# Four graph layers on one core: node terms split into eight gated stages, own rings for the float32r copies, score rows sent by chunk

## The chip, the cores and the metric

The kernel runs on one core of a Trainium2 chip. The metric is the device time of one execution in microseconds (us). Before the change three runs took 3625.14, 3625.96 and 3626.26 us; the median is 3625.96 us. Five engines work side by side, each through its own queue in order: TensorE (PE, with weight loads shown as PEld), VectorE (DVE), ScalarE (ACT), GpSimd (POOL) and SyncE (SP), which here only issues DMAs. POOL issues DMAs too.

## What is computed

x is 3327 x 512, adj a 3327 x 3327 0/1 matrix. Each of four layers normalises the rows, applies a relu, and adds its result to x. Layers 0 to 2 are graph attention with 8, 4 and 8 heads; layer 1 sets the self-loops; layer 3 is a mean over the neighbours with dense weights. Cut to what matters:

```python
h = jnp.maximum(_layernorm(x, axis=-1), 0.0)
Wh = h @ W                                   # per head
f1, f2 = (Wh * a1).sum(-1), (Wh * a2).sum(-1)
e = leaky_relu(f1[:, None] + f2[None, :], 0.2)
att = softmax(where(adj > 0, e, -big), axis=-1)   # layer 1: adj + eye
x = x + elu(att @ Wh)
# layer 3
agg = (adj > 0) @ h / max(deg, 1)
x = x + relu(concat([h @ Ws + bs, agg @ Wn + bn]) @ Wc + bc)
```

## The kernel before

The 3327 rows are 26 tiles of 128; four tiles make a chunk (seven chunks, the last has two). A leaky relu of a sum is one of two products, exp(f1)exp(f2) or its 0.2 power, so attention is two masked sums: of "positive" and of "negative" pairs. A head of a chunk goes like this in `attention` (L540). ACT, and DVE for some columns, compares the row scores s1b with a column's own (L593, L590) and writes 0/2 as fp8. DVE ands it with the mask (L599) and, in layers 0 and 2, makes the other half by xor (L603). PE multiplies these 128 x 128 weights with the exponentiated node terms (`ab`, three bf16 pieces of 65 columns each; L631, L634). Two row tiles `k` are one pass; a head has two passes.

Layer 1 has four heads and takes the positive sum (a = 0) and the negative one (a = 1) in separate passes, 16 a chunk. Its 26 columns lie in five groups of kinds "bssvv": group 0 is multiplied in bf16 (L627), groups 1 and 2 are turned to float32r by ACT, groups 3 and 4 by DVE (`real`, L522, copy at L527), and then multiplied at L624. All four copies of a pass use one ring `t6` of four slots. Between a = 0 and a = 1 DVE flips the masks' half in place (L659).

While layer l attends to chunk c, the rows of chunk c - 1 are finished and become terms of layer l + 1. That is done by `Hooks` (L502): after each pass `run` pushes every flying tile one stage further, starts a new tile every third hook (every hook in the last chunk), and in layer 0 loads one or two blocks of the mask (`load_mask`, L202). A tile's stages (`node_stages`, L428) are: `s0`, finish the row (L727 to L731), statistics on DVE (L301, L303), three small POOL steps (L304 to L306) and the relu on ACT (L308); a stage with nothing; `s1`, four PE transposes (L137) and the copy `hT` on ACT (L141); `s2`, `project` (L351): 8 float32 matmuls (L362), clipped scores (L363), two exponentials on ACT (L369, L370), products (L373) and the pieces on DVE, ACT and POOL (L335 to L341, or L381 and L382); `s3`, the stores and `send_s1` (L420), which transposes one tile's scores (L423), copies them (L425) and writes 8 or 4 rows to DRAM (L426). The head's load at L561 reads them back for 128 partitions.

The framework's scheduler sets the order of each engine's queue from the order of issue, the data dependences, its own notion of durations, and the extra edges that `after` (L144) adds; such an edge orders instructions and is no wait on the chip. `gone` holds the last matmul of each pass.

`open_layer` (L254) is called in the second head of chunk 0. It loads the next layer's weights and folds the two score vectors into them: eight times a product (L291) and a sum (L292), for layers 1 and 2 all on DVE. `mask_tiles` (L231) loads a chunk's masks in the head before the last; for layer 1 POOL copies the self-loop blocks into them at once (L243). Before the first pass of layer 0 the 26 tiles pass through the same stages with nothing beside them but mask loads (the first 172 us, "the lead-in" below).

Of the kernel before, what the change touches and what calls it, by code (L numbers as in the profile page):

```python
# [37 lines left out]
P = 128  # L38
# [14 lines left out]
def tile_gnn(ctx: ExitStack, tc: tile.TileContext, x, adj, W0, a01, W1, al, ar, W2, a2,  # L53
# [48 lines left out]
    s1d = [dram.tile([H, NT * P], F32, name=f"s1_{l}") for l, H in enumerate(heads)]  # L102
# [31 lines left out]
    def transposed(src, pool, name, bufs=2, behind=None):  # L134
        tp = ps.tile([P, KC, P], F32, name="tp", bufs=2)
        for k in range(KC):
            tr = nc.tensor.transpose(tp[:, k, :], src[:, k * P:(k + 1) * P], ident)  # L137
            if k == 0 and behind:
                after(tr, behind)
        dst = pool.tile([P, KC, P], F32, name=name, bufs=bufs)  # L140
        nc.scalar.copy(dst, tp)  # L141
        return dst
# [8 lines left out]
    stats = []  # L151

# [78 lines left out]
    def mask_tiles(c, self_loops=False, early=False):  # L231
        t0, nt = chunks[c]
        tiles = []
        for g, (j0, nj) in enumerate(JG):
            m = mk.tile([P, PER * JM * P], FP8, name="m")
            v = m[:, :nt * nj * P].rearrange("p (k j i) -> p k j i", k=nt, j=nj)
            ld = nc.sync.dma_start(v, maskd[c][g])
            if early and c == 0:
                after(ld, stored[21])
            if self_loops:  # L240
                for k in range(nt):
                    if j0 <= t0 + k < j0 + nj:
                        nc.gpsimd.tensor_copy(v[:, k, t0 + k - j0, :].bitcast(U32), dg1[:, t0 + k, :].bitcast(U32))  # L243
            tiles.append(v)
        return tiles
# [8 lines left out]
    def open_layer(l):  # L254
        L = Layer()
        L.l = l
        L.to_store = []
        if l == 3:
            L.w = []
            for i in range(2):  # L260
                w = pre.tile([P, KC, 2 * WW], F32, name="w")[:, :, :D]
                after(nc.sync.dma_start(w, Xd[i].rearrange("(c p) o -> p c o", p=P)), stored["gate"])
                L.w.append(w)
            return L
        H = heads[l]
        DK = D // H
        H2 = H // 2

        w = pre.tile([P, KC, 2 * WW], F32, name="w")[:, :, :2 * (D // 2 + H)]
        L.w = w.rearrange("p c (f o) -> p c f o", f=2)  # L270
        av = []
        for i in range(2):
            av.append(pre.tile([P, 2, H2, DK], F32, name="h"))
            ld = nc.sync.dma_start(av[i].rearrange("p f h d -> p (f h) d"), a_srcs[l][i].partition_broadcast(P))
            if l:
                after(ld, stored["gate"])
        for k in range(KC):
            for f in range(2):
                dst = L.w[:, k, f, :D // 2]
                if l == 0:  # L280
                    nc.sync.dma_start(dst.rearrange("p (g o) -> p g o", g=H2),
                                      W0[f * H2:(f + 1) * H2, k * P:(k + 1) * P, :].rearrange("h p o -> p h o"))
                else:
                    W = (W1, W2)[l - 1]
                    ld = nc.sync.dma_start(dst, W[k * P:(k + 1) * P, f * (D // 2):(f + 1) * (D // 2)])
                    if l:
                        after(ld, stored["gate"])
        for i in range(2):
            for k in range(KC):
                pr = pre.tile([P, 2, H2, DK], F32, name="e" if l or i else "AB", bufs=1)  # L290
                (nc.gpsimd if l == 0 and i else nc.vector).tensor_mul(pr, L.w[:, k, :, :D // 2].rearrange("p f (g o) -> p f g o", g=H2), av[i])  # L291
                nc.vector.tensor_reduce(L.w[:, k, :, D // 2 + i * H2:D // 2 + (i + 1) * H2], pr, AX.X, ALU.add)  # L292
        L.ks2 = pre.tile([P, NT, H], F32, name="ks2")
        L.ns2 = pre.tile([P, NT, H], F32, name="ns2")
        L.s12 = pre.tile([P, NT, 2, H], F32, name="s12", bufs=1)
        nc.vector.memset(L.s12, 0.0)
        return L

    def norm(xt, pool):
        st = pre.tile([P, 6], F32, name="st")  # L300
        nc.vector.bn_stats(st, xt)  # L301
        mv = pre.tile([P, 4], F32, name="mv")
        stats.append(nc.vector.bn_aggr(mv[:, 0:2], st).ins.name)  # L303
        nc.gpsimd.tensor_scalar(mv[:, 2:3], mv[:, 1:2], EPS, None, op0=ALU.add)  # L304
        nc.gpsimd.tensor_tensor(mv[:, 2:3], mv[:, 2:3], neghalf, ALU.pow)
        nc.gpsimd.tensor_scalar(mv[:, 3:4], mv[:, 0:1], mv[:, 2:3], -1.0, op0=ALU.mult, op1=ALU.mult)  # L306
        h = pool.tile([P, D], F32, name="h", bufs=2)
        nc.scalar.activation(h, xt, AF.Relu, bias=mv[:, 3:4], scale=mv[:, 2:3])  # L308
        return h
# [7 lines left out]
    def pieces(L, t, AB, pool, first):  # L317
# [17 lines left out]
        nc.vector.tensor_sub(r, AB, high(AB))  # L335
        for a in range(2):
            nc.scalar.copy(dst(0, a), high(AB[:, a]))
# [13 lines left out]
    def project(L, t, hT, pool, first):  # L351

        l, n = L.l, pn(t)
        c, kk = where[t]
        g, jj = jwhere[t]
        H, DA, AO, HW = dims(l)
        DK, H2 = DA - 1, H // 2
        pws = []
        for f in range(2):
# [3 lines left out]
            nc.vector.tensor_scalar(L.s12[:n, t, :, f * H2:(f + 1) * H2],  # L363
# [3 lines left out]
        s2 = L.s12[:, t, 1, :]  # L367
        AB = pool.tile([P, 2, H, DA], F32, name="AB", bufs=2 if first else 1)
        nc.scalar.activation(AB[:, 0, :, DK], s2, AF.Exp)  # L369
        nc.scalar.activation(AB[:, 1, :, DK], s2, AF.Exp, scale=SLOPE)  # L370
        for f in range(2):
# [3 lines left out]
                                 AB[:, :, hs, DK:DA].to_broadcast([P, 2, H2, DK]))  # L375
        if l == 1 and KIND[g] != "b":
            for f in range(2):
# [3 lines left out]
                nc.scalar.copy(v[:, 0], AB[:, :, hs])  # L381
# [3 lines left out]
        else:  # L385
            pieces(L, t, AB, pool, first)
        if t == JG[g][0] + JG[g][1] - 1:
            js = slice(JG[g][0], t + 1)
            nc.vector.tensor_scalar(L.ks2[:, js], L.s12[:, js, 1, :], BIG, None, op0=ALU.mult)
            nc.vector.tensor_scalar(L.ns2[:, js], L.s12[:, js, 1, :], -1.0, None, op0=ALU.mult)  # L390
# [29 lines left out]
    def send_s1(L, t, pool, first):  # L420
        H = heads[L.l]
        tps = ps.tile([H, P], F32, name="mm" if first else "tp", bufs=2)
        nc.tensor.transpose(tps, L.s12[:, t, 0, :], ident)  # L423
        s1t = pool.tile([8, P], F32, name="s1t", bufs=2)
        nc.scalar.copy(s1t[:H], tps)  # L425
        (nc.sync if first else nc.gpsimd).dma_start(s1d[L.l][:, t * P:(t + 1) * P], s1t[:H])  # L426

    def node_stages(L, t, get_x, pool, first=False):  # L428
# [4 lines left out]
        def s0():  # L433
            q["h"] = norm(get_x(), pool)

        def s1():
            behind = (L.mm if t == NT - 1 and not first else gone[-1]) if gone else None
            q["hT"] = transposed(q["h"], mp, "A", A_BUFS[2], behind) if late else transposed(q["h"], pool, "hT", 2, behind)

        def s2():  # L440
            if L.l == 3:
                project_last(L, t, q["hT"], 1)
            else:
                project(L, t, q["hT"], pool, first)

        def s3():
            if L.l != 3:
                for to, pt in L.to_store:
                    nc.sync.dma_start(to, pt)
                L.to_store = []  # L450
                send_s1(L, t, pool, first)
            elif late:
# [3 lines left out]
        return [s0, s1, s2, s3] if first else [s0, lambda: None, s1, s2, s3]  # L456

    def close_terms(L):
# [3 lines left out]
        s2v = L.s12[:, :, 1, :].rearrange("p t h -> p h t")  # L462
# [21 lines left out]
        s1v = L.s12[:, :, 0, :]  # L484
# [14 lines left out]
    class Hooks:  # L499


        def __init__(self):  # L502
            self.masks, self.tiles, self.flying, self.done = [], [], [], 0

        def run(self, every, n, masks=1):
            for st in list(self.flying):
                st.pop(0)()
                if not st:
                    self.flying.remove(st)
            if self.tiles and n % every == 0:  # L510
# [11 lines left out]
    def real(a, g, ks, th):  # L522
# [3 lines left out]
        t = mp.tile([P, 2, JM, P], F32R, name="t6", bufs=4)  # L526
# [13 lines left out]
    def attention(L, hooks, open_next, close):  # L540
# [5 lines left out]
        for c, (t0, nt) in enumerate(chunks):  # L546
# [4 lines left out]
            for h in range(H):  # L551
# [9 lines left out]
                nc.sync.dma_start(s1b[:, :W], s1d[l][h, t0 * P:t0 * P + W].partition_broadcast(P))  # L561
# [19 lines left out]
                for g, (j0, nj) in enumerate(JG):  # L581

                    pt = mp.tile([P, PER * JM * P], FP8, name="tht", bufs=11 if l == 1 else 7)
# [24 lines left out]
                for a in range(2 if l == 1 else 1):  # L608
# [5 lines left out]
                    for ks, js in passes:  # L614
# [40 lines left out]
                        hooks.run(1 if last else 3, hook, 2 if hook % 2 and c == 0 or hook % 3 == 0 and c else 1)  # L655
                        hook += 1
                    if a == 0:
                        for pu, mu in flip:
                            nc.vector.tensor_tensor(pu, pu, mu, ALU.bitwise_xor)  # L659
                if c == 0 and h == 0:  # L660
# [14 lines left out]
                if h == H - 2 and not last:  # L675
                    while l == 0 and hooks.done < (t0 + nt + chunks[c + 1][1]) * len(JG):
                        hooks.masks.pop(0)()
                    nmasks = mask_tiles(c + 1, l == 1)
# [74 lines left out]
    with tc.tile_pool(name="first", bufs=1) as fp:  # L753
# [21 lines left out]
        while hooks.tiles or hooks.flying:  # L775
# [8 lines left out]
            [A[1], ("ab", JM * 258, F32R, 7), R, ("t6", 2 * JM * P, F32R, 4), tht[:3] + (11,)],  # L784
# [533 lines left out]
```

## Time and profile before

| what | value |
|---|---|
| median of the runs | 3625.96 us |
| the profiled execution | 3629.69 us |
| its span, first to last instruction | 3627.9 us |
| around the span | 1.8 us |
| mean granted TensorE clock | 0.987 |
| matmuls | 31348 |
| lead-in, layer 0 | 0 to 172.5 us, 172.5 to 1181 us |
| layer 1, layer 2 | 1266 to 2080 us, 2167 to 3200 us |
| layer 3 after the last node terms | 3302 to 3627.9 us |

In the profile a line of a group names the source line, the engine, the operation, the tile written and the tiles read, then the count, the busy time and the mean duration. "Idle before" is time in which that engine stood still, and the arrow names what ended it. A matmul's shown duration includes its way through the array; the next one starts before it ends, so the pace is read from runs of them: 40 float32r matmuls of 258 columns take 5.10 us in a row.

### The profile page before, as it was taken

What the parts mean: (1) busy time and instruction counts of PE and PEld (TensorE: products, weight loads), DVE (VectorE), ACT (ScalarE), POOL (GpSimd) and SP (SyncE); (2) the same over time, 40 slices, a digit from 0 to 9 for tenths busy, and PEclk for the clock granted to TensorE, in tenths of its full rate; (3) what the DMA queues carried; (4) which work ended last, traced back from release to release, by engine and by line L of the source; (5) the groups of instructions that cost most, each with busy time, mean ns of one, the idle gap of its engine ahead of it and who ended that gap; (6) DMA issues with size and microseconds to landing.
All of it is one profiled execution on the core that took longest, in us unless ns stands there. A gap on an engine that the chain in (4) does not pass through costs nothing. (4 is left out here: it accounts for less than half of the span.)

```text
span 3627.9 us, 78882 instructions
## 1 busy us (share of the span) xinstructions
PE 3479.3 (96%) x31348; PEld 3143.1 (87%) x31348; DVE 2642.1 (73%) x5227; ACT 2517.0 (69%) x4170; POOL 620.6 (17%) x893
## 2 busy tenths in 40 slices
PE   7799999999999999999999989999999999999998
PEld 5699999999999888888888869989898989886886
DVE  7788888888887789878878858767776767672221
ACT  5778787778787889878888757767666767572211
POOL 6601221202010202223123230001010101011000
PEclk9999999999999999999999999999999999999999
DMA  7777677777766877767767885545555555586331
GB/s 217 238 211 233 203 234 214 219 220 237 220 200 212 290 270 280 245 247 268 261 246 254 293 290 204 193 168 189 181 184 172 201 176 174 166 284 250 105 106 52
DMA packets 322106, 780.72 MB, mean 215 GB/s; under 512 B 37122, under 2 KB 144645, under 8 KB 321088
## 3 DMA queue, kind: packets, MB, share of 16 engines
q1 hardware_dynamic: 292480, 713.17, 57.8%
q0 software_dynamic: 29248, 62.42, 7.1%
q8 instruction: 249, 4.08, 0.4%
q14 instruction: 129, 1.06, 0.1%
HBM read 667.96 MB, written 129.64 MB: 220 GB/s over the span
## 5 line engine op out<-in xcount | busy, mean ns | idle before, releaser
L631 PE MATMUL acc<-ab,tht 128*128 128x195 bf16 (+1 forms) x10816 | 1845.3, 248 | 14.9 <-DVE tht L599 12.0
L634 PE MATMUL acc<-ab,gt 128*128 128x195 bf16 (+1 forms) x10816 | 1844.8, 248 | 10.5 <-ACT gt L593 6.1
L593 ACT ACTIVATE gt<-s1b,ks 128x512 fp8e4<-128x512 f32 (+1 forms) x2464 | 1456.3, 677 | 250.2 <-issue 144.3
L634 PEld LDWEIGHTS <-gt 128*128 128x128 fp8e4 x10816 | 1061.2, 98 | 32.2 <-issue 16.1
L631 PEld LDWEIGHTS <-tht 128*128 128x128 fp8e4 x10816 | 1061.5, 98 | 25.4 <-DVE tht L599 13.3
L624 PE MATMUL acc<-ab,t 128*128 128x258 f32 x4160 | 547.5, 290 | 33.3 <-ACT t L527 29.4
L624 PEld LDWEIGHTS acc<-ab,t 128*128 128x128 f32 x4160 | 522.8, 193 | 47.1 <-ACT t L527 34.2
L599 DVE TENSOR_TENSOR tht<-gt,m 128x768 uint32<-128x768 uint32 (+3 forms) x560 | 447.2, 799 | 143.3 <-ACT gt L593 140.6
L603 DVE TENSOR_TENSOR gt<-tht,m 128x768 uint32<-128x768 uint32 (+3 forms) x560 | 446.8, 798 | 8.2
L527 ACT CAST t<-tht 128x1536 fp32r<-128x1536 fp8e4 x208 | 300.0, 1468 | 60.1 <-DVE tht L659 29.9
L730 POOL TENSOR_TENSOR xt<-xt,e 128x512 f32<-128x512 f32 x72 | 114.0, 1583 | 1240.6 <-DVE e L729 1198.7
L854 PE MATMUL acc<-y,mf 128*128 128x512 f32 x1352 | 309.8, 391 | 1.5 <-DVE mf L849 1.5
L593 ACT ACTIVATE tht<-s1b,ks 128x512 fp8e4<-128x512 f32 (+1 forms) x504 | 306.8, 679 | 1.8 <-DMA s1b<-s 1.8
L590 DVE TENSOR_SCALAR gt<-s1b,ns 128x512 fp8e4<-128x512 f32 (+1 forms) x448 | 213.5, 479 | 123.9 <-PE acc L634 123.8
L854 PEld LDWEIGHTS acc<-y,mf 128*128 128x128 f32 x1352 | 253.6, 188 | 57.6 <-DVE mf L849 1.9
L649 DVE TENSOR_REDUCE R<-acc 128x130 f32<-128x390 f32 x416 | 214.4, 554 | 70.4 <-PE acc L634 69.7
L851 ACT CAST mf<-m 128x768 fp32r<-128x768 fp8e4 (+1 forms) x78 | 59.1, 762 | 244.9 <-PE acc L854 233.1
L627 PE MATMUL acc<-ab,tht 128*128 128x387 bf16 x1248 | 225.2, 329 | 3.9 <-DMA ab<-ab 2.2
L362 PE MATMUL mm<-w,hT 128*128 128x260 f32 (+1 forms) x832 | 199.3, 392 | 13.5 <-ACT hT L141 10.9
L362 PEld LDWEIGHTS mm<-w,hT 128*128 128x128 f32 x832 | 156.8, 194 | 38.5 <-ACT hT L141 11.8
L627 PEld LDWEIGHTS <-tht 128*128 128x128 fp8e4 x1248 | 118.4, 98 | 80.7 <-DMA ab<-ab 2.2
L339 POOL TENSOR_TENSOR pt<-r 128x520 bf16<-128x520 f32 (+1 forms) x116 | 136.0, 1192 | 285.0 <-DVE r L335 282.6
(139 smaller groups left out, 3164.9 us busy)
## 6 DMA issues: line engine op xcount, KB each, us to landing
ab<-ab SPq DMA_DIRECT2D x336, 600.0 KB
ab<-ab SPq DMA_DIRECT2D x224, 400.0 KB
ab<-ab SPq DMA_DIRECT2D x112, 774.0 KB
ab<-ab SPq DMA_DIRECT2D x112, 516.0 KB
ab<-ab SPq DMA_DIRECT2D x56, 582.0 KB
s1b<-s SPq DMA_DIRECT2D x120, 256.0 KB
m<-mask SPq DMA_DIRECT2D x72, 384.0 KB
ab<-pt SPq DMA_DIRECT2D x13, 1600.0 KB
```

The source lines that it names most:

```text
L362: L.mm = nc.tensor.matmul(pw, hT[:, k, :], L.w[:, k, f, :], start=(k == 0), stop=(k == KC - 1)).ins.name
L527: (nc.scalar.copy if KIND[g] == "s" else nc.vector.tensor_copy)(t[:, :k1 - k0, :nj], th[a][g][:, k0:k1])
L590: nc.vector.tensor_scalar(gv[:, :, jj, :], s1v, L.ns2[:, j, h:h + 1], 2.0, op0=ALU.is_gt, op1=ALU.mult, saturate=False)
L593: nc.scalar.activation(gv[:, :, jj, :], s1v, AF.Relu, bias=L.ks2[:, j, h:h + 1], scale=BIG, saturate=False)
L599: nc.vector.tensor_tensor(pu, gu, mu, ALU.bitwise_and)
L603: nc.vector.tensor_tensor(gu, pu, mu, ALU.bitwise_xor)
L624: mm = nc.tensor.matmul(acc[k][:, :2 * DA], thr[g][:, k - ks[0], jj, :], ab[a][g][:, jj, :], start=(j == 0), stop=(j == NT - 1), skip_grou ...
L627: mm = nc.tensor.matmul(acc[k][:, :3 * DA], th[a][g][:, k, jj, :], ab[a][g][:, jj, :3 * DA], start=(j == 0), stop=(j == NT - 1), skip_grou ...
L631: nc.tensor.matmul(acc[k][:, :3 * DA + o], th[0][g][:, k, jj, :], ab[0][g][:, jj, :3 * DA + o], start=(j == 0), stop=False, skip_group_che ...
L634: mm = nc.tensor.matmul(acc[k][:, AO:AO + 3 * DA + o], th[1][g][:, k, jj, :], ab[0][g][:, jj, AO:AO + 3 * DA + o], start=False, stop=(j == ...
L649: nc.vector.tensor_reduce(R[:, k], v.rearrange("p a (s d) -> p a d s", s=3), AX.X, ALU.add)
L854: nc.tensor.matmul(acc[k], mf[:, jj, :], y2[g][:, jj, s, :], start=(j0 + jj == 0 and s == 0), stop=(j0 + jj == NT - 1 and s == 1))
```

## The change

1. A node tile has eight stages in layers 0 to 2 (six where the next layer is 3): load and finish; statistics; relu; transposes; projection; exponentials and products; pieces; send. From the second on they carry an `after` edge to the last pass's last matmul on their leading instructions (not on every one: the second exponential and the `hT` copy have none). In a layer's last chunk two stages are run per hook.
2. `send_s1` acts once a chunk: one transpose of up to 32 score rows, one copy, one DMA. The scores' DRAM tile is now `[tile, head, row]`, so the read for a head takes 512-byte pieces where it took 2048-byte ones.
3. The eight folds of layers 1 and 2 go one per hook.
4. Layer 1's ring `t6` of four becomes `ts` (three slots, ACT) and `tv` (two smaller slots, DVE); `tht` goes from 11 slots to 10.
5. Layer 1's self-loop copies are issued after the last head's passes.

```diff
-    s1d = [dram.tile([H, NT * P], F32, name=f"s1_{l}") for l, H in enumerate(heads)]
+    s1d = [dram.tile([NT, H, P], F32, name=f"s1_{l}") for l, H in enumerate(heads)]
...
             if self_loops:
                 for k in range(nt):
                     if j0 <= t0 + k < j0 + nj:
-                        nc.gpsimd.tensor_copy(v[:, k, t0 + k - j0, :].bitcast(U32), dg1[:, t0 + k, :].bitcast(U32))
+                        loops.append((v[:, k, t0 + k - j0, :].bitcast(U32), dg1[:, t0 + k, :].bitcast(U32)))
...
+    def set_loops(loops, behind=None):
+        for to, d in loops:
+            cp = nc.gpsimd.tensor_copy(to, d)
+            if behind:
+                after(cp, behind)
...
+        def fold(i, k):
+            pr = pre.tile([P, 2, H2, DK], F32, name="e" if l or i else "AB", bufs=1)
+            m = (nc.gpsimd if l == 0 and i else nc.vector).tensor_mul(
+                pr, L.w[:, k, :, :D // 2].rearrange("p f (g o) -> p f g o", g=H2), av[i])
+            if gone:
+                after(m, gone[-1])
+            nc.vector.tensor_reduce(L.w[:, k, :, D // 2 + i * H2:D // 2 + (i + 1) * H2], pr, AX.X, ALU.add)
+        folds = [lambda i=i, k=k: fold(i, k) for i in range(2) for k in range(KC)]
+        if l:
+            hooks.small = folds
...
-        tps = ps.tile([H, P], F32, name="mm" if first else "tp", bufs=2)
-        nc.tensor.transpose(tps, L.s12[:, t, 0, :], ident)
-        s1t = pool.tile([8, P], F32, name="s1t", bufs=2)
-        nc.scalar.copy(s1t[:H], tps)
-        (nc.sync if first else nc.gpsimd).dma_start(s1d[L.l][:, t * P:(t + 1) * P], s1t[:H])
+        tps = ps.tile([PER * H, P], F32, name="mm" if first else "tp", bufs=2)
+        nc.tensor.transpose(tps[:nt * H], L.s12[:, 0, t0:t0 + nt, :].rearrange("p t h -> p (t h)"), ident)
+        s1t = pool.tile([PER * 8, P], F32, name="s1t", bufs=2)
+        nc.scalar.copy(s1t[:nt * H], tps[:nt * H])
+        (nc.sync if first else nc.gpsimd).dma_start(s1d[L.l][t0:t0 + nt].rearrange("t h p -> (t h) p"), s1t[:nt * H])
...
-        return [s0, s1, s2, s3] if first else [s0, lambda: None, s1, s2, s3]
+        if first:
+            return [lambda: (q.update(x=get_x()), statistics(), relu()), turn,
+                    lambda: parts(L, t, scaled(L, t, projected(L, t, q["hT"], first), pool, first), pool, first), send]
+        stages = [lambda: q.update(x=get_x()), statistics, relu, turn]
+        if L.l == 3:
+            return stages + [lambda: project_last(L, t, q["hT"], 1), own]
+        return stages + [lambda: q.update(pw=projected(L, t, q["hT"], first)),
+                         lambda: q.update(AB=scaled(L, t, q["pw"], pool, first, behind())),
+                         lambda: parts(L, t, q["AB"], pool, first, behind()), send]
...
-        def run(self, every, n, masks=1):
+        def run(self, every, n, masks=1, steps=1):
             for st in list(self.flying):
-                st.pop(0)()
+                for _ in range(min(steps, len(st))):
+                    st.pop(0)()
                 if not st:
                     self.flying.remove(st)
+            if self.small:
+                self.small.pop(0)()
...
-        t = mp.tile([P, 2, JM, P], F32R, name="t6", bufs=4)
+        t = mp.tile([P, 2, nj, P], F32R, name="ts" if KIND[g] == "s" else "tv", bufs=3 if KIND[g] == "s" else 2)
...
-                    pt = mp.tile([P, PER * JM * P], FP8, name="tht", bufs=11 if l == 1 else 7)
+                    pt = mp.tile([P, PER * JM * P], FP8, name="tht", bufs=10 if l == 1 else 7)
...
-                        hooks.run(1 if last else 3, hook, 2 if hook % 2 and c == 0 or hook % 3 == 0 and c else 1)
+                        hooks.run(1 if last else 3, hook, 2 if hook % 2 and c == 0 or hook % 3 == 0 and c else 1, 2 if last else 1)
...
+                if h == H - 1 and not last:
+                    set_loops(pending, gone[-2])
```

## The prediction

> **What bounds the kernel.** First the page's busy shares, then the busy time of each engine by stage (columns: stretch, length, then busy time and instructions of PE, PEld, DVE, ACT, POOL, then granted clock, DMA share, GB/s).
>
> ```profile
> PE 3479.3 (96%) x31348; PEld 3143.1 (87%) x31348; DVE 2642.1 (73%) x5227; ACT 2517.0 (69%) x4170; POOL 620.6 (17%) x893
> ```
>
> ```profile
> 0.00:172.50 172.50, 125.24 (x650) 101.28 (x650) 129.26 (x253) 107.81 (x242) 117.27 (x193) 0.96 0.77 227
> 172.50:1181.00 1008.50, 986.57 (x11236) 968.91 (x11236) 839.82 (x1676) 791.63 (x1363) 166.56 (x258) 0.99 0.73 219
> ...
> 1266.00:2080.00 814.00, 781.64 (x5597) 680.95 (x5597) 682.89 (x1274) 667.19 (x918) 183.83 (x215) 0.98 0.73 262
> 2080.00:2167.00 87.00, 71.58 (x419) 56.74 (x417) 54.37 (x121) 49.00 (x86) 32.02 (x48) 0.95 0.91 329
> 2167.00:3200.00 1033.00, 1030.80 (x10731) 942.89 (x10732) 750.91 (x1482) 719.20 (x1199) 81.18 (x119) 1.00 0.54 183
> ```
>
> PE sets the time; layer 2 is PE without a hole (2.2 us idle). So only three things count: PE work removed, PE idle time, and time in which PE's clock is cut. Idle: 47.3 us in the lead-in, 21.9 in layer 0, 32.4 in layer 1, 15.4 between layers 1 and 2. The waits of PE within layer 1 (total, times, longest):
>
> ```profile
> PE acc L624 <- ACT t L527: 26.0, 12, 4.4
> PE acc L624 <- DVE t L527: 3.6, 5, 0.9
> ```
>
> Layer 1 waits for float32r copies. The timeline at one chunk end shows why; ACT's rows, then PE's:
>
> ```profile
> 1590.48 0.82 ACT L308 ACTIVATE h<-xt,mv 128x512 f32<-128x512 f32 x1 [3.88 <-POOL mv L306]
> 1591.20 4.39 ACT L593 ACTIVATE tht<-s1b,ks 128x512 fp8e4<-128x512 f32 x7
> ...
> 1595.69 2.54 ACT L593 ACTIVATE tht<-s1b,ks 128x512 fp8e4<-128x512 f32 x4
> 1598.14 1.15 ACT L337 COPY pt<-AB 128x520 bf16<-128x520 bf16 x2
> 1599.18 1.46 ACT L527 CAST t<-tht 128x1536 fp32r<-128x1536 fp8e4 x1
> 1600.55 1.15 ACT L341 COPY pt<-r 128x520 bf16<-128x520 bf16 x2
> ```
>
> ```profile
> 1600.70 2.11 PE L624 MATMUL acc<-ab,t 128*128 128x258 f32 x12 [3.04 <-ACT t L527]
> ```
>
> ACT stands 3.88 us at a node's relu that POOL has not prepared, then does 11 compares for a later head and two node copies, and only then the cast that PE needs. The same happens at five chunk ends (waits of 4.4, 3.0, 4.1, 4.1 and 2.9 us, 18.5 together). Over the five 20 us stretches around them PE is busy 81.13 of 100 us, and each has a granted clock of 0.91, another 1.8 us lost: 18.9 + 9.0 = 28 us.
>
> **The clock.** After the 3.04 us wait, 1600.60 to 1605.20 ran at 0.63; after a 5.69 us wait, 224.0 to 229.7 ran at 0.51. So a gap of 3 us costs about 1.7 us more. [...]
>
> **The change, part by part.**
>
> *Gated stages and own rings, layer 1.* The ring first. With one ring of four, the cast of group 1 in pass n waits for the last matmul on group 1 in pass n - 1. From there PE has 28 float32r matmuls (groups 2 to 4) and the 12 of bf16: 40 in 5.10 us gives 0.12 each, 12 in 2.14 us gives 0.16, so 3.4 + 2.0 = 5.4 us of cover. With three slots for ACT alone, the cast of group 2 waits for group 1 of the pass before: another 12 x 0.12, 6.8 us; that of group 1 has 10.7. DVE's cover stays at 5.8. Then the load: in the order of the old program the fullest steady interval between ACT's pairs of casts holds 11 compares, four piece copies, a relu, two exponentials and the casts. At the timeline's paces (0.61, 0.52, 0.72, 0.10, 1.37) that is 12.4 us, plus the 3.88 us idle; PE's pass lasts some 8.0 us (40 x 0.12 + 12 x 0.16, and a sixteenth of four nodes' 4.4 us). 12.4 - 8.0 = 4.4 is more than 5.4 less one cast, 3.9. In the order of the new program the fullest steady one has 12 compares, an exponential and the casts, 10.2 us: 2.2 late against 6.8 - 1.5 = 5.3. The relu stands a hook behind its statistics, so the 3.88 us wait should go too. So the chunk ends should close. I leave 4 of the 28 us: **-24**. Of the other 26.0 - 18.5 + 3.6 = 11.1 us of copy waits I take half, since DVE's ring gains nothing: **-5.5**. Ends for both: 0 and -39.
>
> *Folds.* In layer 0 DVE does eight folds in one go:
>
> ```profile
> 221.36 0.67 DVE L292 TENSOR_REDUCE w<-e 128x4 f32<-128x512 f32 x1
> 221.96 0.41 DVE L665 TENSOR_TENSOR R<-R 128x260 f32<-128x260 f32 x1
> 222.30 0.68 DVE L291 TENSOR_TENSOR e<-w,h 128x512 f32<-128x512 f32 x1
> 222.90 0.16 DVE L667 TENSOR_SCALAR rc<-R 128x4 f32<-128x4 f32 x1
> 222.97 0.95 DVE L603 TENSOR_TENSOR gt<-tht,m 128x768 uint32<-128x768 uint32 x1
> ```
>
> The xor at 222.97 that PE needs (it resumes at 224.06 after 5.69 us) stood behind them; they are 8 x (0.68 + 0.67) = 10.8 us. One per hook, 1.35 us in a pass of 8.7, hides in DVE's idle share. Gone: 5.7 us and half of the 5.7 us at 0.51, 2.8: **-8.5** (ends 0 and -8.5). Layer 1's folds cause no row of waiting.
>
> *Score rows by chunk.* 78 transposes become 21, in layers 1 and 2 52 become 14. Four L137 transposes take 0.60 us and one alone 0.27, so a further one costs 0.11: 38 x 0.11 = **-4**. The copies (0.25) and DMA issues (0.53 on POOL) that go lie off PE. The read back has 512 packets of 512 bytes for 128 of 2048; in the trace's packets these take 27 and 84 ns, so 140 loads cost (13.8 - 10.8) x 140 / 16 = 26 us more of each DMA engine's 3628, and each is asked for a head ahead: 0. If a head waited for its row, the nearest row is ACT's wait for s1b, 1.8 us in two times; ends 0 and +5.
>
> *Lead-in.* PE waits 10.0 us before score transposes and 8.8 (16 times) for hT, for the copy stood behind two exponentials; in the new order it mostly stands ahead of them. But between 40 and 120 us the DMA share is 0.82 to 1.01 and DVE busy 73 of 80 us: these set the pace. **-4**, ends 0 and -19.
>
> *Smaller pieces.* `tht` 11 to 10: one group fewer ahead; nearest row the 0.96 us L599 of 27 heads, ends 0 and +26; taken 0, since two heads still fit. Self-loops later: POOL no longer stands 139 us for masks with node steps queued behind (this is inside the terms above); the next head's L599 now waits for four copies of 0.66: ends 0 and +16, taken 0, since the row of such waits is 1.1 us.
>
> *What is new.* In the new order 19 mask transposes in layer 0 need a score tile's place in PSUM that ACT must copy out first, with 0.3 to 1.1 us of PE work between; and 11 projections in the three last chunks, where two stages go at once, follow their own transposes after 0.3 to 1.8 us. The copy takes 0.57. Behind such a wait stands all of PE's queue. Price: the lead-in's 0.55 a time for the same wait; the 11 cost 0.45 each, the 19 nothing: **+5** (ends 0 and, at the 1.5 us below, +45).
>
> Sum: -24 - 5.5 - 8.5 - 4 - 4 + 5 = -41. The profiled execution's 3629.7 becomes 3588.7; it lies 3.7 over the median, so the median becomes **3585**.
>
> **Rivals.**
> 1. *The casts stay late.* ACT's and DVE's work in layer 1 is the same (667 and 683 of 814 us); if bursts only move, the 29.5 us stay: 3614. For it: DVE's ring has no more cover. Against: the order's loads above.
> 2. *More goes.* All 39 of layer 1, the lead-in's 12, and 10 of the 15.4 idle between layers 1 and 2: 3626 - 39 - 8.5 - 4 - 12 - 10 = 3552. Against: the last chain there (5.66 us for one hT) is a true dependence.
> 3. *Slower: PE behind the hT copies.* The 30 new places, if ACT has three compares (0.61 each) before the copy: about 2 us a time, 60 us, so -46 + 60: 3640. It decides from 46 / 30 = 1.5 us a time. For it: compares come in runs of 7 (4.39 us). Against: in layer 0 ACT idles 217 of 1008 us, and the order puts most copies after a gap.
> 4. *Nothing that counts moves*: the relu still waits for POOL and the folds for their weights: 3626.
>
> **Chances.** Forecast 0.55 (3568 to 3604), rival 1 0.17, rival 2 0.14, rival 3 0.10, rival 4 0.04. A measurement of this kernel tells about 0.2%, 7 us. Faster: the first three less a quarter of rival 1, 0.82; same 0.08; slower 0.10. From 3546 to 3620 lie the forecast, nearly all of rival 1 and four fifths of rival 2: 0.82.
>
> **What would show it.** Right: PE's wait L624 for ACT under 8 us, clock 1.00 at the chunk ends, no gap near 224 us, layer 1 near 785 us. Wrong: casts with 3 us waits still there (rival 1); new rows of PE mask transposes or projections waiting for hT, over 20 us in sum (rival 3).

## The result

The changed kernel took 3609.94 us (median of seven runs, 3601.06 to 3615.72), the kernel before beside it 3626.26 (seven runs, 3622.09 to 3630.14). The ratio is 0.9953 with an interval of 0.9942 to 0.9965: faster by 0.47%. That is inside the forecast's range, but the forecast of 3585 promised 41 us and the medians differ by 16.

The page of the changed kernel; PE is busy 9 us less than before in a span that is 19.8 us shorter:

```profile
span 3608.1 us, 78551 instructions
...
PE 3470.2 (96%) x31291; PEld 3131.4 (87%) x31291; DVE 2648.6 (73%) x5227; ACT 2511.8 (70%) x4113; POOL 603.0 (17%) x855
```

The busy time of each engine by stage of the changed kernel (stretch, length, then busy time and instructions of PE, PEld, DVE, ACT, POOL, then granted clock, DMA share, GB/s). The stretches are cut at the first matmul of each layer:

```profile
0.00:185.10 185.10, 129.00 (x632) 104.52 (x633) 121.61 (x253) 105.62 (x223) 111.04 (x193) 0.92 0.71 211
185.10:1278.00 1092.90, 1065.48 (x11933) 1037.30 (x11933) 904.09 (x1843) 858.40 (x1514) 174.46 (x273) 0.99 0.77 225
1278.00:2143.60 865.60, 842.43 (x5994) 728.47 (x5994) 738.63 (x1393) 716.87 (x983) 215.28 (x245) 0.99 0.78 278
2143.60:3280.30 1136.70, 1123.48 (x11382) 1007.68 (x11382) 820.96 (x1635) 774.85 (x1323) 101.69 (x144) 0.99 0.59 192
```

The same cuts in the kernel before give this balance (us; "gaps" sums what the distance from one matmul to the next exceeds the median distance behind matmuls of the same source line by, where that is over 0.4 us):

| stage | before | after | difference | gaps before, after |
|---|---|---|---|---|
| lead-in | 172.5 | 185.1 | +12.6 | 32.6, 44.0 |
| layer 0 | 1099.7 | 1093.0 | -6.7 | 30.6, 31.5 |
| layer 1 | 901.3 | 865.6 | -35.7 | 51.7, 25.5 |
| layer 2 | 1126.9 | 1136.7 | +9.8 | 9.6, 19.0 |
| aggregation | 327.5 | 327.8 | +0.3 | 2.0, 2.2 |

Each stage is read from one profile. In the runs below whose edit doesn't touch a stage, its length scatters: the changed kernel's lead-in lies between 179.9 and 186.2 us, the other stages within 4 us.

So the change won 42 us in two stages and lost 22 in two others. First the win. PE's waits for the float32r copies in the whole of layer 1 (total, times, longest) were 33 us before:

```profile
PE acc L624 <- ACT t L527: 29.4, 13, 4.4
PE acc L624 <- DVE t L527: 3.6, 5, 0.9
```

They are 2.9 in the changed kernel:

```profile
PE acc L687 <- ACT ts L590: 2.3, 1, 2.3
PE acc L687 <- DVE tv L590: 0.6, 2, 0.4
```

ACT's rows around a relu in the third chunk, the chunk of the rows shown of before:

```profile
1593.12 2.97 ACT L590 CAST ts<-tht 128x1536 fp32r<-128x1536 fp8e4 x2 [0.26 <-PE acc L687]
1595.99 0.21 ACT L401 ACTIVATE AB<-s 128x8 f32<-128x8 f32 x1
1596.10 0.80 ACT L330 ACTIVATE h<-xt,mv 128x512 f32<-128x512 f32 x1
1599.91 2.97 ACT L590 CAST ts<-tht 128x1536 fp32r<-128x1536 fp8e4 x2 [3.01 <-PE acc L687]
```

The relu starts with no idle time ahead of it, and it is the cast that waits for PE to free a slot, not PE for the cast. Over layer 1 ACT's wait for POOL at the relu fell from 38.4 us to 21.3; none of it lies at the five chunk ends any more, and all that is left lies behind 2050 us, in the last chunk.

Now the losses. DVE's wait for tiles of x in the lead-in, first before, then in the changed kernel, where it is the largest:

```profile
DVE st L301 <- DMA xt<-in_x_dram: 2.0, 1, 2.0
DVE st L318 <- DMA xt<-in_x_dram: 26.3, 11, 10.7
```

The rows around the longest of these waits, and what PE had waited for by then:

```profile
120.94 0.17 DVE L322 BATCH_NORM_AGGREGATE mv<-st 128x2 f32<-128x6 f32 x1
131.81 0.69 DVE L318 BATCH_NORM_STATS2 st<-xt 128x6 f32<-128x512 f32 x1 [10.70 <-DMA xt<-in_x_dram]
132.42 1.23 DVE L359 TENSOR_TENSOR r<-AB 128x1040 f32<-128x1040 f32 x1
```

```profile
135.56 6.72 PE L388 MATMUL acc<-w,hT 128*128 128x264 f32 x16 [11.42 <-ACT hT L141]
```

DVE stands 10.7 us at the statistics of the last tile of x, whose load was issued at 117.76. Behind it in DVE's queue is the `r` (L359) of a tile nine places older; ACT waits 11.4 us for that `r`, the hT copy stands behind ACT's wait, and PE behind the copy. In DVE's order a tile's statistics stand eight or nine tiles ahead of the `r` in the changed kernel, and stood six ahead before.

In layer 2 the chief new wait of PE lies at the last chunk:

```profile
3183.75 5.49 PE L443 MATMUL mm<-w,hT 128*128 128x512 f32 x6 [4.80 <-ACT hT L141]
```

```profile
3176.06 4.88 ACT L656 ACTIVATE gt<-s1b,ks 128x256 fp8e4<-128x256 f32 x12
3180.88 0.63 ACT L794 ACTIVATE e<-A 128x512 f32<-128x512 f32 x1
...
3183.14 0.56 ACT L141 COPY hT<-tp 128x512 f32<-128x512 f32 x1
```

A tile's transposes and projection come in one hook there, with nothing of PE's between, and the copy stands behind fifteen compares, twelve of them in a row, and the two steps that finish a row (L794, L795). The matmuls after the wait run at half clock (the windows of the changed kernel around it; the clock is the third figure from the end):

```profile
3184.00:3189.00 5.00, 5.00 (x6) 1.94 (x7) 3.36 (x12) 2.89 (x8) 1.82 (x3) 0.50 0.38 120
```

### The profile page after: what moved, and what is told of

It reads as the page before. It is cut to its first block, busy times and chain, and to the rows that moved or that the text cites. A ratio compares the mean times of both kernels' runs of the same rounds, so it can differ in the third digit from the quotient of the medians.

```text
span 3608.1 us, 78551 instructions
## 1 busy us (share of the span) xinstructions
PE 3470.2 (96%) x31291; PEld 3131.4 (87%) x31291; DVE 2648.6 (73%) x5227; ACT 2511.8 (70%) x4113; POOL 603.0 (17%) x855
## 5 line engine op out<-in xcount | busy, mean ns | idle before, releaser
L590 ACT CAST ts<-tht 128x1536 fp32r<-128x1536 fp8e4 x208 | 300.3, 1471 | 55.9 <-PE acc L687 51.7
L687 PE MATMUL acc<-ab,ts 128*128 128x258 f32 x2496 | 334.2, 290 | 4.4 <-ACT ts L590 2.3
L653 DVE TENSOR_SCALAR gt<-s1b,ns 128x512 fp8e4<-128x512 f32 (+1 forms) x448 | 222.2, 501 | 149.6 <-PE acc L697 147.9
L687 PEld LDWEIGHTS acc<-ab,ts 128*128 128x128 f32 x2496 | 314.1, 191 | 13.4 <-ACT ts L590 3.0
L797 POOL TENSOR_TENSOR xt<-xt,e 128x512 f32<-128x512 f32 x72 | 122.2, 1697 | 888.8 <-DVE e L796 567.5
L687 PE MATMUL acc<-ab,tv 128*128 128x258 f32 x1664 | 220.0, 283 | 3.3 <-DMA ab<-ab 2.2
L687 PEld LDWEIGHTS acc<-ab,tv 128*128 128x128 f32 x1664 | 207.5, 189 | 6.2 <-issue 2.1
```

What stands on the lines that cost most here:

```text
L590: (nc.scalar.copy if KIND[g] == "s" else nc.vector.tensor_copy)(t[:, :k1 - k0, :nj], th[a][g][:, k0:k1])
L653: nc.vector.tensor_scalar(gv[:, :, jj, :], s1v, L.ns2[:, j, h:h + 1], 2.0, op0=ALU.is_gt, op1=ALU.mult, saturate=False)
L687: mm = nc.tensor.matmul(acc[k][:, :2 * DA], thr[g][:, k - ks[0], jj, :], ab[a][g][:, jj, :], start=(j == 0), stop=(j == NT - 1), skip_grou ...
```

## The experiments

Ratios are to the kernel before, run beside each group; the changed kernel's own is 0.9953. Stages are those of the table.

### The lead-in

Theory A: rings of four for statistics let DVE's queue put a tile's statistics too early. B: the score rows sent by chunk. C: the load of the last tile.

**Rings of two for the lead-in's statistics.**

```diff
-        st = pre.tile([P, 6], F32, name="st", bufs=4)
+        st = own.tile([P, 6], F32, name=..., bufs=n)     # lead-in: a ring of its own, n = 2 (mv too)
```

> The changed kernel, but the 26 nodes of the lead-in take their statistics and their mean and scale from rings of two tiles again, not four; later layers keep four. Theory A (the deeper ring lets the scheduler put a node's statistics many places earlier in DVE's queue, where DVE stands 24.4 us in order for x loads that have not landed): the lead-in comes back from 185.1 us to 172 to 176, DVE's waits at the statistics for x loads fall from 24.4 to under 5 us, and the time to about 3598. Rival B (the score rows sent by chunk reorder the lead-in) and rival C (the load of the last, 127-row tile alone): lead-in stays at 183 to 187, time 3608 to 3612.

Lead-in 173.9 us, 3595.22 us, ratio 0.9909 (0.9896 to 0.9923). DVE's wait for x in the whole stage:

```profile
DVE st L319 <- DMA xt<-in_x_dram: 2.0, 1, 2.0
```

The statistics stand six tiles ahead of the `r` again, seven once. A holds for 11.2 of the 12.6 us, give or take the scatter of some 3 us.

**Score rows tile by tile in the lead-in.**

```diff
+        if first:
+            t0, nt = t, 1
-        if k + 1 < nt:
+        elif k + 1 < nt:
             return
```

> The changed kernel, but in the lead-in the score rows are transposed, copied and sent node by node, as before; later layers send by chunk. Rival B: the lead-in falls to 172 to 176 us and the time to about 3598. Theories A and C: the lead-in stays at 183 to 187 (19 more transposes at 0.11 us are 2 us more of PE), time 3608 to 3614.

Between the two: lead-in 178.3 us in the profile, DVE's wait for x still 21.4, ratio 0.9943 (0.993 to 0.9957), which can't be told from the changed kernel's. B is not the cause; at most it moves a few us, and the lead-in's scatter is as large.

**The last tile of x in two pieces.**

```diff
-                nc.sync.dma_start(xt[:pn(u)], x_rows(0, u))
+                cut = pn(u) // 16 * 16
+                nc.sync.dma_start(xt[:cut], x_rows(0, u)[:cut])
+                if cut < pn(u):
+                    nc.sync.dma_start(xt[cut:pn(u)], x_rows(0, u)[cut:])
```

> The changed kernel, but the lead-in's load of the last tile of x (127 rows) goes in two pieces, 112 rows and 15 rows. In the trace its 127 packets trickle over one DMA engine for some 14 us (share 0.06 of 16), and DVE stands 10.7 us at its statistics with two older nodes' work queued behind. Theory C: the wait of 10.7 us falls under 3, PE's gap of 4.8 us near 136 us goes, lead-in 175 to 179, time 3600 to 3604. Theory A alone: the other waits of DVE for x (13.7 us in nine) stay, and the lead-in keeps at least 4 us over the 172.5 of before; if the long load were no cause at all, 183 to 187 and 3610.

Lead-in 175.3, longest wait of DVE for x 3.9 (15.7 in nine), ratio 0.9911 (0.9897 to 0.9924). C holds as well: either mending takes most of the loss, since the early statistics hurt most where the load is slow.

**Both edits.**

> Both: rings of two for the lead-in's statistics and the last tile of x loaded as 112 and 15 rows. Theory A with C: the lead-in is shorter than that of the kernel before, 166 to 170 us, since the 5.6 us gap near 130 us that both kernels show there goes too; time 3592 to 3596. If A holds and C does not, as with the rings alone, 3598. If neither, 3610.

Lead-in 166.0, 3593.7 us, ratio 0.9903 (0.9888 to 0.9918); the profile is 6.5 us below that of before in this stage.

**The split load in the kernel before** (the same edit at L766).

> The kernel before, with nothing changed but the last tile of x in the lead-in loaded as 112 and 15 rows. The kernel before has a gap of PE of 5.6 us near 126 to 132 us, behind a store and a score row that are held up by the one engine that carries the 127 rows. Theory C: the gap goes, with some time at half clock: lead-in from 172.5 to 165 to 168, time 5 to 7 us less than the kernel before. Rival: the load only hurts in the new order, where DVE meets it earlier: lead-in 171 to 174, no change.

Lead-in 166.6, 3618.12 us, ratio 0.9973 (0.9962 to 0.9985). PE's gap of 5.6 us near 130 us in the kernel before is gone. It hung on the same load by another wait: there ACT waited 7.8 us for the store of a score row (1.8 here), not DVE at the statistics.

### Layer 1

**One ring of four again**, with eleven slots for the compares.

```diff
-        t = mp.tile([P, 2, nj, P], F32R, name="ts" if KIND[g] == "s" else "tv", bufs=3 if KIND[g] == "s" else 2)
+        t = mp.tile([P, 2, JM, P], F32R, name="t6", bufs=4)
-                    pt = mp.tile([P, PER * JM * P], FP8, name="tht", bufs=10 if l == 1 else 7)
+                    pt = mp.tile([P, PER * JM * P], FP8, name="tht", bufs=11 if l == 1 else 7)
```

> The changed kernel with the one ring of before for all float32r copies (four slots of six tiles, ACT's and DVE's copies in turn) and eleven slots for the compares; stages, folds and self-loops as changed. By the prediction's own cover sums (2.2 us late against 5.4 less 1.5) theory S, that the stages alone bring ACT's casts in time, gives layer 1 at 865 to 870 us, waits of the float32r matmuls for ACT under 6 us and a time within 5 of 3610. Rival R, that the own rings do it: those waits come back to 12 us or more, layer 1 to 880 or more, time 3624 or more.

Layer 1 875.2, waits for ACT's casts 9.6 us, ratio 0.9978 (0.9968 to 0.9988). Between the theories: the rings are worth some 10 us, the stages the rest. The rings come with one slot fewer for the compares; the two aren't told apart.

**Five stages as before.**

```diff
+        def begin():
+            q["x"] = get_x()
+            q["mv"] = norm(q["x"], pool)
+            q["h"] = normed(q["x"], q["mv"], pool)
...
+        return [begin, lambda: None, turn,
+                lambda: parts(L, t, scaled(L, t, projected(L, t, q["hT"], first), pool, first), pool, first), send]
```

> The changed kernel with a node's work in the stages of before (statistics and relu in one hook, an empty one, the turn, projection with exponentials, products and parts in one, the sending), none of it but the turn behind a matmul, one stage a hook in the last chunk too; own rings, folds, self-loops and score rows as changed. Theory S: ACT again stands some 4 us at the relus and has its compares and copies in a heap, so layer 1 comes back to 885 to 900 us with waits of 2 to 4 us at the chunk ends. Rival R (the rings alone hold): layer 1 at 865 to 872. For the other stages: if the two steps a hook and the gated statistics are what costs layer 2 its 9.8 us, it falls from 1136.7 to about 1128.

Layer 1 914.4, 13 us longer than before the change; layer 2 1124.3; ratio 1.0043 (1.0026 to 1.0059). Theory S (the stages do it), and more than it said. PE's waits in layer 1 of this kernel:

```profile
PE acc L698 <- ACT ts L601: 17.4, 11, 3.4
PE acc L698 <- DVE tv L601: 11.6, 11, 3.9
PE acc L698 <- DMA ab<-ab: 10.5, 5, 3.8
PE mm L388 <- ACT hT L141: 10.5, 4, 7.3
```

**The rings alone in the kernel before** (the last diff the other way round, at L526 and L583).

> The kernel before with nothing changed but the own rings (three slots for ACT's float32r copies, two for DVE's, ten slots for the compares). By the prediction's cover sums the rings alone lengthen ACT's cover from 5.4 to 6.8 us, so the waits of 29.4 us for ACT's casts fall to some 18 to 23 and layer 1 from 901 to 890 to 895; time 3615 to 3620. Rival, from the run with the stages of before and the rings, whose layer 1 was 914 us: with node work in a heap the own rings and the tenth compare slot cost more than they bring, DVE's copies with only two slots become late (11.6 us in that run), layer 1 at 900 to 915, time 3625 to 3640.

The rival holds: layer 1 909.4, waits for ACT's casts down from 29.4 to 17.9, but for DVE's up from 3.6 to 8.6; ratio 1.0037 (1.0023 to 1.0051). Alone the rings cost 8 us in layer 1; beside the new stages they bring 10.

**Statistics and relu in one hook.**

```diff
-        stages = [lambda: q.update(x=get_x()), statistics, relu, turn]
+        stages = [lambda: q.update(x=get_x()), lambda: (statistics(), relu()), lambda: None, turn]
```

> The changed kernel, but a node's statistics and its relu share one hook (with an empty hook after it), so that the relu stands in ACT's queue straight behind statistics that DVE and POOL still have to do; projection, exponentials with products, and parts keep a hook each. The prediction laid the late casts to two causes: ACT standing 3.9 us at the relu (cause 1) and the heap of node work between two pairs of casts (cause 2). If cause 1 weighs most: layer 1 from 865.6 to 890 or more and the waits for float32r copies above 12 us. If cause 2: layer 1 at 866 to 874.

Layer 1 888.0, layer 0 1120.8, ratio 1.0101 (1.0084 to 1.0118): this one regrouping undoes the whole change and more. ACT's wait at the relu in layer 1 of this kernel, and then PE's at the mask transposes in layer 0, which was 6.9 us in the changed kernel:

```profile
ACT h L330 <- POOL mv L325: 52.5, 26, 7.9
```

```profile
PE tp L221 <- ACT hT L141: 22.2, 8, 7.1
```

**Projection, exponentials and parts in one hook.**

```diff
-        return stages + [lambda: q.update(pw=projected(...)), lambda: q.update(AB=scaled(...)), lambda: parts(...), send]
+        return stages + [lambda: parts(L, t, scaled(L, t, projected(...), ...), ...), lambda: None, lambda: None, send]
```

> The changed kernel, but projection, exponentials, products and parts share one hook (with two empty ones after it); statistics, relu and turn keep a hook each. If the heap (cause 2) weighs most: layer 1 at 885 or more. If the relu (cause 1): 866 to 874.

Layer 1 855.7, 10 us **shorter** than in the changed kernel, layer 0 1098.1, ratio 0.994 (0.9924 to 0.9957). The heap costs layer 1 nothing: PE's waits for the casts are 6.9 us there against 2.9, but its waits for loads of `ab` fell from 7.1 to 2.4, and it idles 17.6 us against 23.1.

**The relu alone, in the kernel before.**

```diff
         def s0():
-            q["h"] = norm(get_x(), pool)
+            q["x"] = get_x()
+            q["mv"] = norm(q["x"], pool)
+        def relu():
+            q["h"] = normed(q["x"], q["mv"], pool, gone[-1] if gone else None)
...
-        return [s0, s1, s2, s3] if first else [s0, lambda: None, s1, s2, s3]
+        return [lambda: (s0(), relu()), s1, s2, s3] if first else [s0, relu, s1, s2, s3]
```

> The kernel before with one thing changed: a node's relu comes a hook after its statistics, in the hook that was empty, and behind the last matmul of that pass; one ring, folds, self-loops, score rows and all other stages as before. If cause 1 (ACT standing at the relu) explains layer 1: its waits for ACT's casts fall from 29.4 us to under 12, layer 1 from 901 to 870 to 885, time 3600 to 3612. If the relu's own hook only helps together with the other gated stages or the own rings: layer 1 at 892 or more, time 3618 or more.

3578.81 us, ratio 0.9864 (0.9848 to 0.9881): this one move is worth nearly three times the whole change. The relu also gets an edge to the pass's last matmul here; in the run with statistics and relu in one hook it had that edge and the time was lost, so the edge alone doesn't do it. Whether the hook alone does wasn't tried. Its windows for layers 0, 1 and 2:

```profile
170.00:1253.60 1083.60, 1067.56 (x11953) 1041.84 (x11954) 901.62 (x1842) 862.49 (x1533) 192.38 (x293) 0.99 0.76 228
1253.60:2120.30 866.70, 845.21 (x6015) 729.26 (x6012) 736.05 (x1393) 716.34 (x1004) 215.87 (x262) 0.99 0.78 277
2120.30:3240.80 1120.50, 1115.04 (x11383) 1004.64 (x11381) 809.93 (x1636) 771.38 (x1320) 102.12 (x145) 1.00 0.59 194
```

Layer 1 has all but 1 us of the changed kernel's gain, with the old ring; PE's waits for its casts there fell from 33 to 8.3:

```profile
PE acc L633 <- ACT t L536: 6.4, 10, 2.1
...
PE acc L633 <- DVE t L536: 1.9, 5, 0.5
```

ACT's wait for POOL at the relu in layer 1, before and in this run:

```profile
ACT h L308 <- POOL mv L306: 38.4, 17, 4.8
```

```profile
ACT h L311 <- POOL mv L306: 10.7, 4, 4.8
```

In layer 0 it fell from 26.0 to 5.2. Layer 0 is 16 us shorter, layer 2 is 6 shorter, and the aggregation is 5 longer.

**Self-loops at once**, as before.

```diff
-                    nmasks, loops = mask_tiles(c + 1, "later") if l == 1 else (mask_tiles(c + 1), [])
+                    nmasks, loops = mask_tiles(c + 1, l == 1), []
```

> The changed kernel with layer 1's self-loops copied into a chunk's masks as soon as the masks are asked for, as before, so that POOL stands for the masks with the node steps queued behind it; all else as changed. Theory: the relus of the chunk ends then stand behind POOL's mean and scale again, ACT's casts are late, and layer 1 comes back by 5 to 20 us (871 to 886), with waits of the float32r matmuls for ACT above 6 us; time 3615 to 3630. Rival: the own rings carry the late casts anyway, or the later copies cost the next head as much as they bring: layer 1 at 862 to 868, time 3608 to 3612.

Layer 1 868.4, ratio 0.9952 (0.9936 to 0.9969): the rival, no effect that can be told.

### Folds and last chunks

**Folds in one go.**

```diff
-            if gone:
-                after(m, gone[-1])
...
-        if l:
-            hooks.small = folds
-        else:
-            for f in folds:
-                f()
+        for f in folds:
+            f()
```

> The changed kernel with the folds of the score vectors for the next layer in one go, as before, not one a hook. By the prediction's term: the gap of some 5.7 us near the start of layer 0 comes back with its time at half clock, layer 0 from 1093 to 1100 or 1102, layer 1 the same, time 3617 to 3619. Rival: the xor that PE waits for no longer stands behind them, as the order has moved otherwise, or the gap is made up later: layer 0 within 2 of 1093, time 3610.

Layer 0 1099.0, ratio 0.9975 (0.9964 to 0.9986). The gap is back, at its old size:

```profile
PE acc L692 <- ACT gt L651: 5.7, 1, 5.7
```

**One stage a hook in the last chunk too.**

```diff
-                        hooks.run(1 if last else 3, hook, ..., 2 if last else 1)
+                        hooks.run(1 if last else 3, hook, ..., 1)
```

> The changed kernel with one stage of each node a hook in the last chunk as well, not two. Theory: the last chunk's projections no longer follow straight on their own transposes, the 5.0 us gap at the end of layer 2 and the waits for copies of the last chunks of layers 0 and 1 (about 9 us in sum) go: layer 2 at 1128 to 1131, time about 3600. Rival: the last chunk has eight hooks and a node needs eight and starts up to three hooks late, so nodes are left over when the chunk ends and their chain of transpose, copy and projection stands open between the layers: 3 to 6 us longer at each end of a layer, time 3618 or more.

Layer 2 1122.1, layer 0 1096.8, ratio 0.9933 (0.9913 to 0.9953). The tail of layer 2 (first the changed kernel, then this one): 9 us of idle time become 1.3, and the clock stays full. The second window holds more of the stage's matmuls.

```profile
3165.00:3280.30 115.30, 106.22 (x792) 78.25 (x789) 66.13 (x178) 66.21 (x146) 21.56 (x35) 0.96 0.77 278
```

```profile
3160.00:3268.60 108.60, 107.31 (x874) 83.76 (x872) 72.46 (x192) 71.35 (x162) 25.69 (x37) 1.00 0.82 309
```

### Together

**Both mendings of the lead-in and one stage a hook in last chunks.**

> The three mendings together: statistics rings of two in the lead-in, the last tile of x as 112 and 15 rows, one stage a hook in the last chunk too. Theory (they lie in different stages and add up): lead-in 166 us, layer 0 1094 to 1098, layer 1 865, layer 2 1122, aggregation 328, together 3575 to 3579; ratio to the kernel before about 0.987. If the clock or the stores shift what one gains to another: 3590 or more.

3585.92 us, ratio 0.9884 (0.9868 to 0.9901); lead-in 162.8, layer 0 1099.9, layer 2 1122.1. That is some 7 us over the expected sum: layer 0 and the aggregation (331.4) are longer than the single edits had them.

**The same, one stage a hook in layer 2 alone.**

```diff
+                        hooks.run(1 if last else 3, hook, ..., 2 if last and l < 2 else 1)
```

> As the run before, but one stage a hook in the last chunk of layer 2 alone; layers 0 and 1 keep two. If the 3.8 us that layer 0 grew by with one stage everywhere are real, this is some 4 us faster than the run with one stage everywhere; if they are scatter of one profile, the two are within 3 us.

3580.7 us, ratio 0.9869 (0.9853 to 0.9885); layer 0 1092.8. The two agree within their intervals; the profiles show no gain from one stage a hook in layers 0 and 1. All these edits of the changed kernel together reach what the relu alone brought the kernel before (0.9864).

**And projection to parts in one hook.**

> The changed kernel with statistics rings of two in the lead-in, the last tile of x as 112 and 15 rows, one stage a hook in layer 2's last chunk, and projection, exponentials, products and parts in one hook in all layers. If the 10 us that the shared hook brought layer 1 are real and add up: layer 1 at 854 to 858, layer 0 some 4 longer, together 3572 to 3577, ratio 0.986 or less. If they were scatter of one profile: layer 1 at 862 to 868, time 3580 or more.

3573.89 us, ratio 0.9839 (0.9821 to 0.9857); layer 1 854.8, layer 0 1103.4.

**The shared hook for the nodes of layer 2 alone** (`if L.l == 2`; these run within layer 1).

> As the run before, but the shared hook only for the nodes of layer 2, whose work runs within layer 1; the nodes worked in layers 0 and 2 keep a hook for each of the three. If the gain is layer 1's and the 5 us that layer 0 grew by belong to the shared hook there: layer 0 at 1093, layer 1 at 854 to 858, time 3568 to 3573. If neither is real: 3580.

3569.02 us, ratio 0.9834 (0.9818 to 0.9851), the fastest of all; layer 1 855.6, layer 0 1093.4. The 10 us of the shared hook held three times.

## Why the prediction was right and wrong

**The lead-in: wrong, -4 against +12.6.** The step that failed is "between 40 and 120 us the DMA share is 0.82 to 1.01 and DVE busy 73 of 80 us: these set the pace", from which both ends were at or below nothing. In the changed kernel DVE is busy 56.5 us of the same stretch: it stood in order behind loads. The change of the statistics' rings from two to four, which neither the list of the change nor the prediction has, set this off; undone, the stage is back at 173.9. The sum has no term for it. The old ring had kept a late load's consumer from standing further ahead of older work. The -4 for hT copies that stand ahead of the exponentials isn't there either: with the load split, the new order with rings of two takes 166.0 and the old one 166.6. Between these two PE's waits for score transposes fell from 4.5 to 0.3 us, but those for hT rose from 8.1 to 13.6.

**What is new: too small.** Of the 19 mask transposes ("the 19 nothing") ten wait, 8.3 us in sum, and the last chunks' projections cost more than 11 x 0.45: two stages a hook account for layer 2's 9.8 us, as one brings 14.6 back. The largest single wait is rival 3's mechanism, with the compares ahead of the copy as it said: fifteen of them from 3176 us on, 4.80 us instead of 2. The flat price of 0.45 a time came from the lead-in, where no compares stand in ACT's queue.

**Layer 1: right in place and cause, the size -35.7 for -29.5 and some -2 of score transposes.** Of the two reasons given, one was right: "ACT stands 3.88 us at a node's relu that POOL has not prepared". The relu's own hook alone gives -34.6 in this stage, without the rings. The other, the load in one interval, fails: with projection to parts in one hook the stage is shorter still. So do the cover sums: they make the old ring enough for the new stages, and it costs 10 us there; they make the own rings a gain for the old stages, and alone they lose 8. "DVE's ring gains nothing" was right, but DVE lost: its waits grew from 3.6 to 8.6 with rings alone. Why the shared hook helps layer 1 is open.

**Layer 0: folds right, the relu missed.** The folds' -8.5 is 4 to 6 us in the stage, by the scatter of layer 0, and 8 in the ratio. But the relu's move alone took 16 us off layer 0 as well (12 or 13 beside the two other edits of that kernel, whose layer 0 took 1095.9 and 1096.7), in which the prediction saw no wait of this kind since PE's rows there name mask loads, a self-block product and compares, not ACT's stand. Of the relu and the folds together only 6.7 us are left in the changed kernel. New waits of the mask transposes explain about 8; the rest of it is open. Whether the relu, the folds and the split load together in the kernel before would do as well as the best combination wasn't tried.

**The small terms.** Score transposes, -4: the sum of the usual distances between matmuls fell by some 2 us in layer 0 and 2 in layer 1, right. Self-loops at nothing: right. The 512-byte reads at nothing: no run undoes them alone; ACT's waits for these rows are 6.1 us in the changed kernel against 1.8, and no wait of PE is put down to them. Rival 1 (casts stay late) is refuted by the 2.9 us, rival 4 by the windows. On the clock the prediction's reading of the rows was right: in the trace of before, PE's gaps of 2.95 us (up to 2000.99) and 1.97 us (up to 1341.44) were each followed by 3.4 us at a clock of 0.50, so 1.7 us were lost at each.

**The sum** failed by 16.6 us in the lead-in, some 4 in layer 0 and 7 in layer 2, and was made up for by 6 in layer 1.

## What to carry to other kernels

When a change has many parts, look for the instruction on an in-order engine that waits for another engine's short work; moving that one consumer a step later can be the whole gain (here the relu alone gave 0.9864, the whole change 0.9953), and the rest has to be measured for what it takes back. A deeper ring is an edit to price: it lets a scheduler put an instruction that waits for a slow load in front of work that is ready (here DVE's waits for x in the lead-in went from 2.0 us to 26.3). Where two dependent steps of PE lie in one slot, the price is what stands in the copying engine's queue at that place (here 4.80 us), not the copy's duration (0.56).

## What the runs showed of the hardware

The last tile of x, 127 rows of 2048 bytes, trickled: in the last stretch before it landed, the changed kernel's DMA engines ran 26 packets in 2 us at 25 GB/s, 6.5% of sixteen engines, as much as one of them. From issue at 117.76 to the statistics at 131.81 it took 14 us at most, where loads of 128 rows took 5.5 (median of two). As 112 and 15 rows, it left DVE's longest wait for x in the changed kernel at 3.9 us, and PE's gap of 5.6 us in the kernel before was gone. Why 127 rows trickled is not shown by any run.

PE's wait of 4.80 us was followed by 5 us at a clock of 0.50, 2.5 us lost, so that its price was about half as much again. With one stage a hook layer 2 has no half clock left (15.1 us of it in the changed kernel).
